# A two-layer graph attention kernel: the write of q's halves and the load of the next tile's q stack are issued at a later place of SyncE's queue

## The chip, the cores and the metric

The kernel runs on one core of a Trainium2 chip. The core has a matrix engine (TensorE: PE for matmuls, PEld for the loads of their stationary operand), a vector engine (VectorE, DVE), a scalar engine (ScalarE, ACT), a general-purpose engine (GpSimd, POOL), and SyncE (SP), which here only issues DMAs. Each engine runs its own list of instructions in order and waits on semaphores for the others. DMAs are issued from SyncE's queue (q1 in the profile) and from GpSimd's (q0); the bytes of both are moved by the same 16 DMA engines.

The metric is the device time of one execution in microseconds. Before the change it is 3294.1 us, the median of three executions (3287.58, 3294.10 and 3294.34). In the text a "slot" is one turn of the kernel's main loop, a "step" is one of the eight turns of the loop inside it, and "+x" is a time in us after a slot's first score matmul.

## What is computed

The reference takes node features x (16 graphs, 1024 nodes, 256 features) and an integer adjacency matrix of each graph, and applies two layers, each of which adds its output to x.

```
# layer 0: attention with 8 heads of 32
h = relu(layernorm(x))
Q, K, V = h @ Wq.T + bq, h @ Wk.T + bk, h @ Wv.T + bv        # by head
scores = where(adj == 0, -inf, Q @ K.T / sqrt(32))
x = x + (softmax(scores) @ V) @ Wo.T + bo

# layer 1: attention of one head, its scores chosen by the kind of the edge
h = relu(layernorm(x))
e_k = leaky_relu((h * a_k) @ h.T, 0.2)                       # k = 0..3
scores = e_0 where adj == 1, e_1 where 2, e_2 where 3, e_3 where 4, else -9e15
x = x + softmax(scores) @ h
```

The adjacency given here holds zeros and ones. The kernel notes while it runs whether any other kind occurs, and only then computes layer 1 a second time for all kinds.

## The kernel before

**Slots.** A graph (the batch index b) has 8 tiles of 128 query nodes, so there are 128 tiles. The main loop is a software pipeline over slots s. In slot s, `now` is the tile s whose attention is computed; `was` and `gone` are the two tiles before it, whose output is being finished; `nxt` is tile s + 1, whose inputs are being fetched; `edge` and `edge_was` are tiles of layer 1, which runs nine tiles behind; `piece`, `piece_was` and `piece_nxt` are tiles of the projections, which run about nine tiles ahead. In slot s, `piece_was` is tile s + 8. The loop over h inside a slot has one step for each head. The order of the instructions is written by hand (`tc.manual_schedule()`): on each engine and each queue they run in the order of the program.

**The projections.** For each piece the keys and queries are projected in two chunks of 128 output features (`project`, line 261). ScalarE then writes the result, rounded to a type that TensorE reads in one pass, into the first half of a `halves` buffer (`high`, line 277), and VectorE writes the remainder into the second half (`split`, line 282). The tag `halves` has four buffers: two are used for the keys of a piece and two for its queries. The key halves are made at the end of step 7 and split at steps 0 and 1 of the next slot. The query halves are made at step 5 and split at step 6.

The halves go to DRAM. The keys are written twice, by SyncE's queue right at the split and by GpSimd's a little later (line 309), into `kd`. The queries are written by `write_queries` (line 303) into `qd`, once for each chunk, with each half repeated: 256 KB a DMA. Before the change it is called at step 7.

**Loads.** For the scores of a tile, TensorE needs the q stack `qt`: 128 partitions (32 head dimensions by high and low half by two copies) by 8 heads by 128 queries, 512 KB in pieces of 512 bytes. `load_queries` (line 390) reads it from `qd` on SyncE's queue into one of two buffers. Before the change it is issued for `nxt` at step 1. The stack of tile s + 1 is loaded in slot s, and the halves that were made in slot s belong to tile s + 8. The keys of a whole graph (eight loads of 512 KB, line 344) stay in place for eight slots. The next graph's are loaded on GpSimd's queue during the last slot of a graph and the first of the next: one at step 3, one at the end of step 4, one at the start of step 5, one at the end of step 6, then at steps 0, 2, 3 and 4. GpSimd's queue also loads the adjacency tile (line 394, 512 KB, step 4).

**Scores and softmax.** At each step TensorE computes the scores of one head (line 423, two matmuls), VectorE adds the mask and takes the row extremum (line 435), and ScalarE takes the exponential (line 443).

**Turning the probabilities.** For the product with V the probabilities of a head must lie transposed. Heads 2, 3, 6 and 7 are transposed by TensorE (line 543) and copied by ScalarE (line 544). Heads 0, 1, 4 and 5 (`BY_BLOCKS`) take another way: VectorE transposes blocks of 32 by 32 (line 364), and four DMAs of 128 KB on SyncE's queue (line 369, `place_blocks`) move the blocks to their partitions in a buffer `pT`. Head h is turned two steps after its scores, so heads 0 and 1 are moved at steps 2 and 3 and heads 4 and 5 at steps 6 and 7. The edge tile's probabilities are moved the same way at step 0.

**The products.** `combine(0)` (line 478; 64 matmul instructions of a call in the profile) multiplies heads 0 to 3 with V at step 7, after the scores of head 7. `combine(1)` does heads 4 to 7 at step 3 of the next slot. `gather` (line 609) does the same for the edge tile at steps 5 and 6, and its result leaves through `store`: VectorE's `ot` (line 618) and SyncE's DMA `out` (line 619), at step 6. The residual row goes out at step 6 as well (`x1d`, line 504).

**SyncE's queue in a slot.** Because a queue runs in order, the order of its DMAs matters for the change. In the kernel before, from step 0 on, it is: one key write, four moves of the edge tile, one key write, the q stack, four moves of head 0, four of head 1, the output, four moves of head 4, the residual row, four moves of head 5, two q writes. That is 27 DMAs, and the profile shows about 0.6 us of the queue for each.

Of the kernel before, what the change touches and what calls it, by code (L numbers as in the profile page):

```python
# [42 lines left out]
def gnn_kernel(  # L43
# [138 lines left out]
    class Piece:  # L182
# [116 lines left out]
                self.queries.append((oc, halves))  # L299

        def write_queries(self):
            for oc, halves in self.queries:
                nc.sync.dma_start(
                    out=qds[self.b][self.first, oc].rearrange("p u w n -> p u (w n)"),
                    in_=halves.unsqueeze(1).to_broadcast([P, 2, 2 * P]),
                )
# [34 lines left out]
    def load_key(b, h):  # L341
        kt = keys.tile([P, N], F32R, tag=f"k{h}", name=f"k{h}_{b}")
        c, r = divmod(h, GROUP)
        (nc.sync, nc.gpsimd)[b > 0].dma_start(
            out=kt.bitcast(F32),
            in_=kds[b][c, r * HD : (r + 1) * HD].rearrange("d w u n -> (d w u) n"),
        )
        keysets.setdefault(b, {})[h] = kt
# [178 lines left out]
    def norms(tile_0, piece):  # L527

        both = [(a, x) for a, x in ((tile_0, tile_0 and tile_0.x1), (piece, piece and piece.x[:, 0, :])) if a]
        if both:  # L530
            mv = stats_place(len(both))
            for i, (_, xt) in enumerate(both):
                stats_of(xt, mv[:, i, :])
            r, shift = norm_of(mv)
            for i, (a, _) in enumerate(both):
                a.norm = r[:, i : i + 1], shift[:, i : i + 1]
# [151 lines left out]
    def attend_of(s):  # L688
        return Attend(*divmod(s, NT)) if 0 <= s < B * NT else None

    def edges_of(s):
        s -= LAG
        return Edges(*divmod(s, NT)) if 0 <= s < B * NT else None

    def piece_of(s):
        s += LEAD
        return Piece(*divmod(s, NT)) if s < B * NT else None

    with tc.manual_schedule():
        first = [Piece(0, 0, 4), Piece(0, 4, 4)]  # L700
        piece_was = Piece(1, 0)
# [6 lines left out]
        nxt = attend_of(1)  # L708
# [16 lines left out]
        piece, edge, edge_was = piece_next, None, None  # L725
# [6 lines left out]
            piece_was.project(0, oc)  # L732
            piece_was.high()

        gone = was = None
        for s in range(B * NT + LAG + 1):
            b, t = divmod(s, NT)

            def load_keys(h, end):
                if t == NT - 1 and b + 1 < B and 2 * h + end in KEY_STEPS:  # L740
                    load_key(b + 1, KEY_STEPS.index(2 * h + end))
                if t == 0 and 0 < b < B and 2 * (HEADS + h) + end in KEY_STEPS:
                    load_key(b, KEY_STEPS.index(2 * (HEADS + h) + end))

            nxt2, edge_nxt, piece_nxt = attend_of(s + 2), edges_of(s + 1), piece_of(s + 1)
            for h in range(HEADS):
                ending, eh = (now, h - 1) if h >= 1 else (was, HEADS - 1)
                turning, th = (now, h - 2) if h >= 2 else (was, HEADS + h - 2)

                load_keys(h, 0)  # L750


                if now:
                    now.scores(h)
                if h == 0 and piece_was:
                    piece_was.split()
                if h == 1 and piece_was:
                    piece_was.split()
                if h == 2 and edge:
                    edge.softmax_max()  # L760
                if h == 5:
                    if was:
                        was.residual()
                    norms(was, piece_nxt)
                if h == 6 and edge_was:
                    edge_was.gather(1)
                if h == 6 and piece_was:
                    piece_was.split()
                    piece_was.split()
                if now:  # L770
                    now.softmax_max(h)
                if h == 6 and edge_was:
                    edge_was.store()
                if h == 4 and edge:
                    edge.leak()


                if ending:
                    ending.softmax_exp(eh)

                if h == 1 and gone:
                    gone.turned_normed()


                if h == 3:
                    if piece_was:
                        piece_was.project(1, 0)
                        piece_was.project(1, 1)
                    if was:
                        was.combine(1)  # L790
                    if piece_was:
                        piece_was.biased()
                    if was:
                        was.combined()
                if turning and th in BY_BLOCKS:
                    turning.turn_blocks(th)
                    turning.place_blocks(th)
                elif turning:
                    turning.turn(th, 0)
                    turning.turn(th, 1)  # L800


                if h == 0:
                    if piece_was:
                        piece_was.write_again()
                    if edge:
                        edge.score(0)
                    if gone:
                        gone.turn_normed()
                    if edge_was:  # L810
                        edge_was.turn_blocks()
                        edge_was.place_blocks()
                if h == 1:
                    if edge:
                        edge.score(1)
                    if was:
                        was.reciprocals()
                    if piece_nxt:
                        piece_nxt.load()
                    if piece_was:  # L820
                        piece_was.write_again()
                    if nxt:
                        nxt.load_queries()
                if h == 2:
                    if piece_was:
                        piece_was.values()
                    if was:
                        was.turn_reciprocals()
                        was.turned_reciprocals()
                        was.add_bias()  # L830
                    if edge_was:
                        edge_was.load_nodes()
                if h == 3:
                    if nxt:
                        nxt.flag()
                        nxt.mask()
                if h == 4:
                    if was:
                        was.output()
                    if piece:  # L840
                        piece.normed()
                    if edge_nxt:
                        edge_nxt.prepare()
                    if nxt2:
                        nxt2.load()
                if h == 5:
                    if edge_was:
                        edge_was.gather(0)
                    if piece:
                        piece.turn()  # L850
                    if piece_was:
                        piece_was.high()
                        piece_was.high()
                    if piece:
                        piece.turned()
                if h == 6:
                    if edge:
                        edge.softmax_exp()
                    if was:
                        was.keep()  # L860
                    if now:
                        now.load_nodes()
                    if piece:
                        piece.project(0, 0)
                        piece.project(0, 1)
                if h == 7:
                    if now:
                        now.combine(0)
                    if piece_was:
                        piece_was.write_queries()  # L870
                    if piece:
                        piece.high()
                        piece.high()
                    if was:
                        was.normed()
                load_keys(h, 1)
            gone, was, now, nxt = was, now, nxt, nxt2
            edge_was, edge = edge, edge_nxt
            piece_was, piece = piece, piece_nxt


        seen = small.tile([P, B], F32, tag="seen", bufs=1)
# [49 lines left out]
```

## Time and profile before

| what | value |
|---|---|
| median of three executions | 3294.1 us |
| the profiled execution | 3310.8 us, its span 3309.0 us |
| mean granted TensorE clock | 0.979 of full speed |
| PE busy | 3080.0 us, 93% of the span |
| VectorE busy | 2802.7 us, 85% |
| ScalarE busy | 2458.4 us, 74% |
| GpSimd busy | 1735.3 us, 52% |
| DMA | 762.93 MB, 231 GB/s; q1 takes 55.3% and q0 19.9% of the 16 engines' span |

Busy time is the time in which an engine runs instructions; waiting for semaphores and issuing DMAs is not counted. A row of a group gives the line, the engine, the operation, what it writes and reads, how often, then the busy time and the mean ns of one, then the idle time of the engine just before these instructions and what ended most of it. A row of a DMA issue gives the size and the median time from issue to landing. A row of the timeline gives the start, the duration, the engine, the line, the operation and how many were merged, with the idle time before them in brackets. A row of the stage table gives a stretch of time, its length, the busy time of PE, PEld, VectorE, ScalarE and GpSimd, then the granted clock, the share of the 16 DMA engines that was busy, and GB/s.

### The profile page before, as it was taken

How to read it: one execution, taken by the hardware profiler on the slowest of the kernel's cores; microseconds unless marked ns; L12 is line 12 of the kernel's file. 1: busy time of each engine (PE TensorE's matmuls, PEld its weight loads, DVE VectorE, ACT ScalarE, POOL GpSimd, SP SyncE). 2: the span in 40 equal slices, each digit the busy share in tenths (PEclk: the TensorE clock that was granted, in tenths of full speed). 3: DMA queues.
4: the chain of work that ended last, by engine and by line, in shares of the span. 5: the costliest groups of instructions: out<-in, count | busy, mean ns of one | idle time of the engine just before them, and what ended most of it. 6: DMA issues, size and time to landing. Idle time of an engine off the chain costs nothing. (4 is left out here: it accounts for less than half of the span.)

```text
span 3309.0 us, 98026 instructions
## 1 busy us (share of the span) xinstructions
PE 3080.0 (93%) x36018; PEld 2239.0 (68%) x36018; DVE 2802.7 (85%) x5111; ACT 2458.4 (74%) x4829; POOL 1735.3 (52%) x3902
## 2 busy tenths in 40 slices
PE   4888999999999999999999999999999999998997
PEld 2666767777676767767677677776766676676653
DVE  2887989989898989989899888989988899898963
ACT  2887878778787877878778777878777788787750
POOL 2555555555555555555555555555555555555531
PEclk9898999999999999999999999999999999999999
DMA  5777787877878787787878878787787877877642
GB/s 187 219 232 227 235 262 221 269 225 235 264 221 267 225 254 241 223 261 228 255 229 240 245 229 253 228 261 237 229 257 218 250 235 231 252 231 242 197 136 70
DMA packets 747063, 762.93 MB, mean 231 GB/s; under 512 B 71280, under 2 KB 692080, under 8 KB 746576
## 3 DMA queue, kind: packets, MB, share of 16 engines
q1 hardware_dynamic: 678288, 542.21, 55.3%
q0 software_dynamic: 65088, 210.16, 19.9%
q8 instruction: 290, 4.75, 0.6%
q10 hardware_dynamic: 3200, 4.19, 0.3%
q14 instruction: 197, 1.61, 0.1%
HBM read 252.98 MB, written 167.77 MB: 127 GB/s over the span
## 5 line engine op out<-in xcount | busy, mean ns | idle before, releaser
L435 DVE CUSTOM_DVE_ANT_0 p<-s,neg 128x1024 f32<-128x1024 f32 x1024 | 1233.6, 1205 | 150.6 <-issue 120.5
L443 ACT ACTIVATE p<-p,nmx 128x1024 f32<-128x1024 f32 x1024 | 1178.4, 1151 | 221.2 <-DVE nmx L435 219.7
L423 PE MATMUL s<-k,qt 128*128 128x512 f32 x2048 | 797.3, 471 | 21.8 <-DVE nmx L435 9.8
L478 PE MATMUL acc<-pT,v 128*32 128x128 f32 x16384 | 561.0, 283 | 112.3 <-DMA pT<-blocks 110.7
L544 ACT COPY pT<-trp 128x512 f32<-128x512 f32 x1024 | 543.8, 582 | 162.6 <-PE trp L543 151.9
L403 POOL TENSOR_SCALAR neg<-adj 128x1024 bf16<-128x1024 int32 x128 | 467.0, 3648 | 359.3 <-ACT neg L415 358.9
L364 DVE STREAM_TRANSPOSE blocks<-p 128x1024 f32<-128x1024 f32 x512 | 632.2, 1235 | 0.1
L478 PEld LDWEIGHTS acc<-pT,v 128*32 128x32 f32 x16384 | 472.1, 114 | 196.8 <-issue 119.4
L543 PE MATMUL trp<-ident,p 128*128 128x128 f32 x4096 | 534.2, 274 | 0.2 <-ACT pT L544 0.2
L543 PEld LDWEIGHTS trp<-ident,p 128*128 128x128 f32 x4096 | 481.0, 141 | 74.0 <-ACT pT L544 3.6
L609 PE MATMUL acc<-h,pT 128*32 128x256 f32 x8192 | 509.9, 383 | 12.5 <-DMA pT<-blocks 11.8
L565 PE MATMUL s<-h1T,ha 128*128 128x512 f32 x1024 | 482.8, 595 | 0.5 <-ACT h1T L522 0.5
L423 PEld LDWEIGHTS s<-k,qt 128*128 128x128 f32 x2048 | 331.1, 192 | 155.0 <-issue 107.7
L609 PEld LDWEIGHTS acc<-h,pT 128*32 128x32 f32 x8192 | 246.6, 110 | 228.5 <-issue 78.0
L462 POOL COPY wide<-rec 128x256 f32<-128x256 f32 x128 | 51.0, 398 | 573.3 <-DVE rec L460 573.3
L309 POOL DMA_DIRECT2D kd<-halves x240 | 169.6, 707 | 238.6 <-DVE halves L282 230.6
L579 DVE CUSTOM_DVE_ANT_0 sel<-s,neg 128x1024 f32<-128x1024 f32 x128 | 156.8, 1225 | 146.2 <-PE s L565 146.2
L565 PEld LDWEIGHTS s<-h1T,ha 128*128 128x128 f32 x1024 | 175.3, 191 | 130.0 <-issue 128.6
L591 ACT ACTIVATE sel<-sel,nmx 128x1024 f32<-128x1024 f32 x128 | 145.5, 1137 | 70.8 <-DVE rec L616 64.9
L443 ACT ACTIVATION_READ_ACCUMULATOR p<-p,nmx 128x1 f32 x1024 | 193.7, 189 | 0.0
L472 ACT COPY recT<-acc 128x256 f32<-128x256 f32 x128 | 47.8, 373 | 176.7 <-PE acc L468 176.7
L261 PEld LDWEIGHTS acc<-hT,wkT 128*128 128x128 f32 x960 | 119.5, 195 | 76.1 <-issue 46.9
(106 smaller groups left out, 4008.3 us busy)
## 6 DMA issues: line engine op xcount, KB each, us to landing
pT<-blocks SPq DMA_DIRECT2D x2560, 128.0 KB, 3.5
qt<-qd SPq DMA_DIRECT2D x128, 512.0 KB, 5.5
adj<-in_adj POOLq DMA_DIRECT2D x127, 512.0 KB, 4.8
qd<-halves SPq DMA_DIRECT2D x240, 256.0 KB, 3.2
k<-kd POOLq DMA_DIRECT2D x120, 512.0 KB, 7.0
kd<-halves SPq DMA_DIRECT2D x240, 128.0 KB, 3.8
kd<-halves POOLq DMA_DIRECT2D x240, 128.0 KB, 3.6
xb<-in_x POOLq DMA_DIRECT2D x128, 128.0 KB, 3.0
```

The source lines that it names most:

```text
L309: queue.dma_start(out=kds[self.b][oc, :, :, twice, self.cols], in_=halves.rearrange("p (w n) -> p w n", w=2),)
L364: nc.vector.transpose(blocks.rearrange("p b j q -> p j b q"), p)
L403: nc.gpsimd.tensor_scalar(self.neg, self.adj, 0.0, MASKED, ALU.is_equal, ALU.mult)
L423: nc.tensor.matmul(self.ps[:, cols], lhsT=self.qt[:, h, :], rhs=keysets[self.b][h][:, cols], start=True, stop=True,)
L435: nc.vector.tensor_tensor_reduce(out=p, in0=sides[h in (3, 5, 7)], in1=self.neg, scale=-SCALE, scalar=FLOOR, op0=ALU.add, op1=ALU.min, acc ...
L443: nc.scalar.activation(p, p, AF.Exp, bias=nmx, scale=-1.0, accum_out=self.sums[:, h : h + 1])
L478: nc.tensor.matmul(sums_place[r * HD : (r + 1) * HD, g * P : (g + 1) * P], lhsT=vs[self.b][:, j, place_of(h) : place_of(h) + HD], rhs=self ...
L543: nc.tensor.transpose(tr[:, j, :], p[:, jj * P : (jj + 1) * P], ident)
L544: copy(pT[:, half * 4 : half * 4 + 4, :], tr)
L565: nc.tensor.matmul(self.e[:, cols], lhsT=self.ha[:, c, :], rhs=h1Ts[self.b][:, c, cols], start=(c == 0), stop=(c == NC - 1),)
L579: nc.vector.tensor_tensor_reduce(out=self.sel, in0=self.e, in1=masks[self.b, self.t], scale=-1.0, scalar=3e38, op0=ALU.add, op1=ALU.min, a ...
L609: nc.tensor.matmul(sums_place[a * HD : (a + 1) * HD, :], lhsT=self.pT[:, j, a], rhs=h1s[self.b][:, j, :], start=(j == 0), stop=(j == NT - 1),)
```

## The change

`write_queries` is no longer called at step 7 of the slot that made the halves. It is called at step 3 of the slot after, right behind the moves of head 1's blocks, for the piece that was `piece_was` one slot ago (`piece_gone`). `load_queries` is no longer called at step 1 but at step 3, directly behind that write and ahead of the mask's two instructions. The loop over a piece's queries now empties the list as it goes.

SyncE's queue in a slot is then: one key write, four moves of the edge tile, one key write, four moves of head 0, four of head 1, two q writes, the q stack, the output, four moves of head 4, the residual row, four moves of head 5. No instruction is added to any engine, and no buffer or size changes.

```diff
         def write_queries(self):
-            for oc, halves in self.queries:
+            while self.queries:
+                oc, halves = self.queries.pop(0)
                 nc.sync.dma_start(
...
-        gone = was = None
+        gone = was = piece_gone = None
...
                     if piece_was:
                         piece_was.write_again()
-                    if nxt:
-                        nxt.load_queries()
                 if h == 2:
...
                 if h == 3:
+                    if piece_gone:
+                        piece_gone.write_queries()
                     if nxt:
+                        nxt.load_queries()
                         nxt.flag()
                         nxt.mask()
...
                 if h == 7:
                     if now:
                         now.combine(0)
-                    if piece_was:
-                        piece_was.write_queries()
...
-            piece_was, piece = piece, piece_nxt
+            piece_gone, piece_was, piece = piece_was, piece, piece_nxt
```

## The prediction

> **What bounds the kernel now.** I read the page's engine shares first, then the list of waits (TensorE's, then SyncE's queue), then the timeline of two slots, then the stage table. A slot is one turn of the main loop (one query tile); its start is its first score matmul, and "+x" is us after that.
>
> ```profile
> PE 3080.0 (93%) x36018; PEld 2239.0 (68%) x36018; DVE 2802.7 (85%) x5111; ACT 2458.4 (74%) x4829; POOL 1735.3 (52%) x3902
> ...
> L478 PE MATMUL acc<-pT,v 128*32 128x128 f32 x16384 | 561.0, 283 | 112.3 <-DMA pT<-blocks 110.7
> ...
> pT<-blocks SPq DMA_DIRECT2D x2560, 128.0 KB, 3.5
> qt<-qd SPq DMA_DIRECT2D x128, 512.0 KB, 5.5
> ```
>
> TensorE is the bound; its one large wait is `combine` (L478) waiting for the moves of blocks. SyncE's timeline shows who is ahead of those moves. An ordinary slot (start 1062.93), then the last slot of a batch, "key slot" (start 1009.12), and TensorE's answer in it:
>
> ```profile
> 1067.50 1.21 SPq L303 DMA_DIRECT2D qd<-halves  x2
> 1068.80 0.58 SPq L309 DMA_DIRECT2D kd<-halves  x1
> 1069.48 3.62 SPq L369 DMA_DIRECT2D pT<-blocks  x4
> 1073.21 0.55 SPq L309 DMA_DIRECT2D kd<-halves  x1
> 1073.86 0.57 SPq L390 DMA_DIRECT2D qt<-qd  x1
> 1074.53 5.26 SPq L369 DMA_DIRECT2D pT<-blocks  x8
> 1084.00 0.60 SPq L619 DMA_DIRECT2D out<-ot  x1
> ```
>
> ```profile
> 1019.83 0.57 SPq L390 DMA_DIRECT2D qt<-qd  x1
> 1020.50 8.21 SPq L369 DMA_DIRECT2D pT<-blocks  x8
> ...
> 1034.95 3.63 PE L478 MATMUL acc<-pT,v 128*32 128x128 f32 x62 [4.21 <-DMA pT<-blocks]
> ```
>
> The eight moves of heads 0 and 1 stand directly behind the 512 KB stack load. In the key slot the stack lands 8.3 us after issue, at 1028.15, and the eighth move is issued at 1028.17: each of SP's DMAs waits for the one eight places ahead. That move lands 6.5 us later, at 1034.7, and `combine(0)` waits for it. The stage table shows what else the stall costs and where DMA has room:
>
> ```profile
> 1081.00:1083.00 2.00, 2.00 (x35) 1.16 (x28) 1.83 (x5) 2.00 (x6) 1.45 (x8) 1.00 0.89 293
> 1083.00:1085.00 2.00, 2.00 (x38) 1.64 (x41) 1.91 (x5) 2.00 (x5) 1.42 (x8) 1.00 0.04 14
> ```
>
> ```profile
> 1025.00:1030.00 5.00, 5.00 (x69) 3.01 (x62) 4.64 (x13) 4.48 (x12) 4.24 (x14) 1.00 1.00 327
> 1030.00:1035.00 5.00, 0.79 (x8) 0.22 (x9) 3.82 (x6) 3.37 (x7) 4.18 (x13) 0.83 0.97 329
> 1035.00:1038.50 3.50, 3.50 (x62) 3.13 (x62) 0.00 (x0) 0.00 (x0) 0.00 (x0) 0.50 0.87 253
> ```
>
> In the ordinary slot the DMA engines fall idle (0.04) from +20 to +22. In the key slot they are full (0.97 to 1.00), and after the stall the granted clock is 0.50: 62 matmuls take 3.63 us, against 2.03 us for 64 in the ordinary slot. So 4.2 us of waiting cost 6.2.
>
> **What there is to win.** A slot without a wait takes 23.18 us. Measured from the starts of the score matmuls, 84 ordinary slots (neither first nor last of a batch) are on average 0.68 longer: 57 us. Fifteen slots (14 last slots, and the one at 249.5) are 6.1 longer: 92. Thirteen first slots of a batch are 1.65 longer: 21. Together 171 us. The slots before and after these hardly wait for moves.
>
> **Part by part.**
> *Load of the q stack, from step 1 to step 3.* No instruction is added. Heads 0 and 1's moves lose 0.6 us of SP's issue and the 512 KB ahead of them. Their blocks are ready at +10.6 and +13.5 (the transposes at 1072.26 and 1075.21, 1.23 us each), so the moves now start at those times and the last is issued at +15.4. A move lands in 3.5 us: +19, and `combine(0)` starts at +21.2. In the key slot only one key load (at +10.4) is beside them; even 5.6 us would do. So the 171 us is taken off whole.
> *Write of q's halves, from step 7 to step 3 of the next slot.* Two DMAs of 256 KB, 1.2 us of SP. What stood behind them (key write, edge moves) is issued 1.2 us earlier; the edge moves are used at +15.1, so this is worth nothing. Now they precede the stack: issued +16.0 and +16.6, the stack at +17.3. Behind these three stands SP's output store, which in the ordinary slot is issued at +21.1 anyway (it waits for VectorE's `ot`): 3.2 us of cover. The stack of the tile written now is read seven slots later, so there is no data wait.
> *The halves' buffers.* Four rotate. ScalarE writes the next q halves at +17.45 (1080.38), when the write of the old ones, issued +16.6, is in flight (3.2 us: until +19.8). If the same buffers came up, ScalarE would stall 2.4 us a slot, and the key projection and two VectorE splits behind it. In the program as compiled before, buffers of a tag go in the order in which they were given back (the seven of pT: 4, 5, 6, 0, 2, 1, 3); the key halves are given back at steps 0 and 1, so q's should take theirs, and the key halves at +21.9 take q's. I price it at nothing and keep the stall as a rival.
> *Where the wait goes.* The stack must land before the next slot's first scores, +23.1: 5.8 us after issue, where it had 12. Its landing is the unknown. Low end: 4.5 us, the fastest of the trace: no wait. High end: 8.1, the median of the key slots' loads, with one 512 KB key load issued within 0.8 us: 2.3 us of wait a slot. The adjacency load, the same 512 KB, is issued on GpSimd's queue at +16.65, 0.7 before the stack, so beside it. What takes me toward the low end is the packets of the stage above: the adjacency load occupies the engines from +18 to +20, then they idle. By the trace's packet records a 512-byte packet takes 27 ns and one of 1 KB 46 ns; the stack is 64 of the first on each engine (1.7 us), a move 8 of the second (0.37 us). At +18 SP's ring then holds about 0.3 us of q writes and the stack, 2.0 us. In before, a ring holding three moves (1.1 us) at that point had landed them 3.1 us later, and one with five (1.9 us) 3.9 to 4.9 later. So the stack lands at +22 to +23.4: I take 0.2 us an ordinary slot: 84 x 0.2 = 17 us.
> *Key slots.* Two key loads go out on GpSimd right behind the adjacency load (1026.35), 1.5 MB from +18 to +24.5. SP's DMAs issued then land 6.5 to 7.1 us later for 128 KB (the moves at 1028.17 and 1033.25). The stack, four times that, lands between +25.4 (8.1 us) and +29: a wait of 2.3 to 5.9, plus up to 1.6 at the half clock. I take 4.0: 15 x 4.0 = 60. First slots have one key load (+16.8) beside adjacency: +24.6 or so, and the old waits for keys: 13 x 2.0 = 26.
> Sum: -171 + 17 + 60 + 26 = -68 us. The profiled execution is 3310.8 us, 16.7 above the median of 3294.1; taken off the median, 3226 us.
>
> Two rules speak to this, and no term above uses them. The Trainium skill, "DMA: Bandwidth & Descriptors", section "Queues, rings and completion order", says that each DMA engine takes turns between queues packet by packet. That speaks against the change: the stack's 512-byte packets would give the 4 KB packets of the adjacency load a full turn each and wait for all of it, some 1.5 us more; the ordinary slots would then cost about 84 x 1.2 = 100 us and the sum would be +15. "TensorE: Matmul & The Clock Gate", section "What's actually happening", puts the halving of the clock at an idle window of about 3.4 us; the new waits in key slots lie on both sides of that, and by it a wait of 2.4 us would cost nothing beyond itself.
>
> **Rivals.**
> *A, the forecast:* most of the wait of `combine` gone, a small one for the stack in its place: 3200 to 3270. Chance 0.42.
> *B, the stack is always in time,* in key slots too (below 2 us there): -171 + 10 to 45: 3130 to 3165. For it: 0.04 of DMA use from +20 to +22. Against: full engines in key slots. 0.13.
> *C, ends slower: the stack comes late in every slot.* Place: the first scores. It decides from 6.8 us of landing on: a 1.0 us wait in 84 slots is 84, and with 60 and 26 the 171 are spent. With 7.3 us (median of the first slots' loads, which have key loads beside them) and key slots as long as now: -171 + 126 + 92 + 40 = +87: 3381; with 8.1, 3448. For it: all loads with a 512 KB neighbour issued up to 3 us earlier took 7 us or more. Against: those rings were full, this one is drained. 0.31.
> *D, the buffers:* ScalarE stalls 2.4 us for the q write in 118 slots: +283 - 68: 3509. 0.07.
> *E, one wait for another:* within 0.2% (about what a measurement of this kernel can tell from no change), 3288 to 3301. 0.07.
>
> **Numbers.** Faster is A and B, 0.55; same is E, 0.07; slower is C and D, 0.38. The time is A's, 3226. The range leaves out D, the upper third of C and the lower part of B: 3160 to 3410; A's own range is 3200 to 3270.
>
> **What would show it.** Right: the row of L478 waiting for pT falls from 110.7 to below 15; stack issues sit at +17 with a median landing of 5 to 6 us; a new wait of L423 for qt, of some us in key slots and under 0.5 in others. Wrong: a median landing near 7 or more and L423 waiting in every slot (C); ScalarE's q halves (L277) waiting for the write of qd (D); L478 still waiting for heads 0 and 1, which would mean that the load ahead was not what held them.

## The result

The changed kernel takes 3440.6 us (median of four executions, 3431.6 to 3447.8); the kernel before took 3294.2 beside it (four, 3287.6 to 3301.1). The ratio is 1.0443, with a 95% interval of 1.041 to 1.0476. The prediction of 3226 us, faster, was wrong; what came is the case that it called C: the stack is late in every slot.

From the page of the changed kernel: the engines' busy shares, then three groups (line, engine, operation | busy time and mean ns | idle time before it and what ended it), then DMA issues with the median us from issue to landing. Lines behind the change have moved down by one (L423 is L424, L478 is L479).

```profile
PE 3087.0 (90%) x36018; PEld 2242.0 (65%) x36018; DVE 2814.4 (82%) x5111; ACT 2463.4 (72%) x4829; POOL 1729.8 (50%) x3902
...
L424 PE MATMUL s<-k,qt 128*128 128x512 f32 x2048 | 801.6, 473 | 244.0 <-DMA qt<-qd 215.2
...
L479 PE MATMUL acc<-pT,v 128*32 128x128 f32 x16384 | 514.7, 275 | 2.7 <-DMA pT<-blocks 1.9
...
L277 ACT ACTIVATE halves<-acc,bk_t 128x128 fp32r<-128x128 f32 x240 | 86.5, 362 | 129.2 <-DMA qd<-halves 124.8
...
pT<-blocks SPq DMA_DIRECT2D x2560, 128.0 KB, 2.9
qt<-qd SPq DMA_DIRECT2D x128, 512.0 KB, 6.8
adj<-in_adj POOLq DMA_DIRECT2D x127, 512.0 KB, 5.4
qd<-halves SPq DMA_DIRECT2D x240, 256.0 KB, 5.6
```

The wait that the change aimed at is gone: `combine` waited 110.7 us for moves and waits 1.9 now. In its place the scores wait 215.2 us for the q stack. TensorE's busy time hardly changed (3080.0 to 3087.0); the span grew from 3309.0 to 3429.7.

By slots, in excess of the 23.18 us of a slot without a wait, for the 110 slots from 9 to 118 in both traces:

| slots | before | after |
|---|---|---|
| 84 ordinary | 57.0 | 132.3 |
| 13 last of a graph (key slots) | 78.0 | 71.7 |
| 13 first of a graph | 21.4 | 69.5 |
| all 110 | 156.5 | 273.5 |

That is 117.0 of the 120.7 us by which the span grew. SyncE's timeline of one ordinary slot of the changed kernel (its first score matmul at 1147.99):

```profile
1162.41 1.91 SPq L370 DMA_DIRECT2D pT<-blocks  x3
1164.37 1.30 SPq L304 DMA_DIRECT2D qd<-halves  x2
1165.71 0.62 SPq L391 DMA_DIRECT2D qt<-qd  x1
```

The order is the one that was foreseen, and the times are within 0.4 us of it: last move at +15.7, q writes at +16.4 and +17.0, stack at +17.7. GpSimd issues the adjacency load in this slot at 1164.63, +16.6. The stage table of the same slot (length; busy time of PE, PEld, VectorE, ScalarE, GpSimd; granted clock; share of the DMA engines that was busy; GB/s):

```profile
1164.00:1166.00 2.00, 2.00 (x28) 1.01 (x24) 1.90 (x6) 1.48 (x5) 1.69 (x5) 1.00 0.79 218
1166.00:1168.00 2.00, 2.00 (x35) 1.11 (x28) 1.84 (x5) 2.00 (x6) 1.43 (x8) 1.00 1.00 214
1168.00:1170.00 2.00, 2.00 (x38) 1.63 (x40) 1.91 (x5) 2.00 (x5) 1.42 (x8) 1.00 0.98 341
```

From +18 to +20 (the second row) the DMA engines are busy the whole time (1.00) and move only 214 GB/s; two microseconds later they move 341 at nearly the same share (0.98). The trace's packet records say whose time that is: from +18.5 to +20.5, SP's queue got 40 packets of 1 KB through, where it had 156 in the half microsecond before; GpSimd's 4 KB packets took 550 ns each at first and 175 at the end of it. Only then did the q writes go on, and behind them the stack's 512-byte packets (27 ns each). The stack landed at +25.5, and TensorE's timeline shows what that costs:

```profile
1173.49 1.22 PE L424 MATMUL s<-k,qt 128*128 128x512 f32 x2 [2.24 <-DMA qt<-qd]
1174.51 1.91 PE L544 MATMUL trp<-ident,p 128*128 128x128 f32 x8
1176.21 2.18 PE L566 MATMUL s<-h1T,ha 128*128 128x512 f32 x4
...
1178.37 0.71 PE L424 MATMUL s<-k,qt 128*128 128x512 f32 x2
1178.92 1.04 PE L544 MATMUL trp<-ident,p 128*128 128x128 f32 x8
1179.79 1.88 PE L566 MATMUL s<-h1T,ha 128*128 128x512 f32 x4
```

After a stall of 2.24 us the same three groups take 1.22, 1.91 and 2.18 us, and one step later 0.71, 1.04 and 1.88: the stall costs another 1.7 us. The stage table has the granted clock at 0.50 there:

```profile
1174.00:1176.00 2.00, 2.00 (x9) 1.71 (x8) 1.15 (x3) 0.40 (x1) 0.00 (x0) 0.50 0.89 261
```

### The profile page after: what moved, and what is told of

The parts are those of the page before. It is cut to its first block, busy times and chain, and to the rows that moved or that the text cites. A ratio compares the mean times of both kernels' runs of the same rounds, so it can differ in the third digit from the quotient of the medians.

```text
span 3429.7 us, 97675 instructions
## 1 busy us (share of the span) xinstructions
PE 3087.0 (90%) x36018; PEld 2242.0 (65%) x36018; DVE 2814.4 (82%) x5111; ACT 2463.4 (72%) x4829; POOL 1729.8 (50%) x3902
## 3 DMA queue, kind: packets, MB, share of 16 engines
q0 software_dynamic: 65088, 210.16, 20.1%
## 4 chain that ended last, share of the span: by engine, by line
PE 54%; DMA 26%; SPq 12%; issue 2%; DVE 1%; ACT 0%; DVEq 0%; ACTq 0%
DMA qt<-qd 25%; PE s L566 12%; PE s L424 11%; PE trp L544 10%; SPq L370 8%; PE acc L479 7%; SPq L304 4%; PE acc L261 3%; PE acc L494 3%; PE acc L329 3%; PE acc L610 2%; DMA pT<-blocks 1%; PE acc L519 1%; PE acc L469 1%; DVE blocks L365 1%
## 5 line engine op out<-in xcount | busy, mean ns | idle before, releaser
L424 PE MATMUL s<-k,qt 128*128 128x512 f32 x2048 | 801.6, 473 | 244.0 <-DMA qt<-qd 215.2
L424 PEld LDWEIGHTS s<-k,qt 128*128 128x128 f32 x2048 | 332.7, 193 | 382.6 <-issue 171.3
L544 PE MATMUL trp<-ident,p 128*128 128x128 f32 x4096 | 558.0, 281 | 0.4 <-ACT pT L545 0.4
L544 PEld LDWEIGHTS trp<-ident,p 128*128 128x128 f32 x4096 | 501.2, 145 | 75.9 <-issue 5.2
L479 PE MATMUL acc<-pT,v 128*32 128x128 f32 x16384 | 514.7, 275 | 2.7 <-DMA pT<-blocks 1.9
L566 PE MATMUL s<-h1T,ha 128*128 128x512 f32 x1024 | 506.4, 620 | 0.5 <-ACT h1T L523 0.5
L479 PEld LDWEIGHTS acc<-pT,v 128*32 128x32 f32 x16384 | 443.3, 110 | 70.7 <-DVE ot L619 38.5
L566 PEld LDWEIGHTS s<-h1T,ha 128*128 128x128 f32 x1024 | 187.2, 203 | 141.5 <-issue 140.2
L277 ACT ACTIVATE halves<-acc,bk_t 128x128 fp32r<-128x128 f32 x240 | 86.5, 362 | 129.2 <-DMA qd<-halves 124.8
```

The lines of the kernel that those rows point to most:

```text
L424: nc.tensor.matmul(self.ps[:, cols], lhsT=self.qt[:, h, :], rhs=keysets[self.b][h][:, cols], start=True, stop=True,)
L479: nc.tensor.matmul(sums_place[r * HD : (r + 1) * HD, g * P : (g + 1) * P], lhsT=vs[self.b][:, j, place_of(h) : place_of(h) + HD], rhs=self ...
L544: nc.tensor.transpose(tr[:, j, :], p[:, jj * P : (jj + 1) * P], ident)
L566: nc.tensor.matmul(self.e[:, cols], lhsT=self.ha[:, c, :], rhs=h1Ts[self.b][:, c, cols], start=(c == 0), stop=(c == NC - 1),)
```

## The experiments

The ring is what SyncE's queue has issued and the DMA engines have not yet moved. Three theories stood at the start. N, the neighbour: SP's writes and the stack are held by the adjacency load beside them. R, the ring: the stack is late because it stands behind 512 KB of writes in SP's ring. P, the place: the DMA engines have no room there for the stack at all. Beside them stood the halves' buffers (the prediction's case D). Each kernel was timed beside the kernel before.

| kernel | stack load | q write | adjacency load | us | ratio to before, 95% interval |
|---|---|---|---|---|---|
| before | step 1 | step 7 | step 4 | 3294.2 | 1 |
| changed | step 3 | step 3 | step 4 | 3440.6 | 1.0443 (1.041 to 1.0476) |
| load alone | step 3 | step 7 | step 4 | 3270.7 | 0.9914 (0.9882 to 0.9945) |
| write alone | step 1 | step 3 | step 4 | 3256.6 | 0.9879 (0.9846 to 0.9911) |
| both, adjacency late | step 3 | step 3 | step 6 | 3252.7 | 0.9859 (0.9843 to 0.9876) |
| adjacency late alone | step 1 | step 7 | step 6 | 3255.7 | 0.9877 (0.9835 to 0.992) |
| stack ahead of the write | step 3 | step 3 | step 4 | 3306.6 | 1.003 (1.0012 to 1.0049) |
| five halves buffers | step 3 | step 3 | step 4 | 3442.2 | 1.0456 (1.0378 to 1.0535) |
| adjacency, half late | step 3 | step 3 | 4 and 6 | 3315.6 | 1.007 (1.005 to 1.009) |
| adjacency in two halves | step 3 | step 3 | 4 and 4 | 3455.8 | 1.0472 (1.0435 to 1.0509) |
| stack at step 0 | step 0 | step 7 | step 4 | 3320.0 | 1.0073 (1.0046 to 1.01) |
| stack at 0, write at 3 | step 0 | step 3 | step 4 | 3225.1 | 0.9783 (0.9745 to 0.9822) |
| the same, adjacency late | step 0 | step 3 | step 6 | 3252.3 | 0.9888 (0.9865 to 0.9912) |

**One part alone.** The load moved without the write:

```diff
-                    if nxt:
-                        nxt.load_queries()
                 if h == 2:
...
                 if h == 3:
                     if nxt:
+                        nxt.load_queries()
                         nxt.flag()
```

> The stack load alone moves to step 3; q's halves are written at step 7 as before. Theory R (the ring): the stack comes late because the two q writes, 512 KB, stand right ahead of it on SyncE's ring, and are themselves held by the adjacency load; without them the stack is issued at about +16.2 instead of +17.8, lands in 5.3 to 5.8 us, by +22, and TensorE's wait for qt (215 us in the changed kernel) falls below 40: 3170 to 3230 us. Theory N (the neighbour): any 512 KB load beside the adjacency load takes about 6.7 us; it lands at +22.9 to +23.5 and waits a little in every slot: 3240 to 3310 us, qt's wait 60 to 130. Theory P (the place): the DMA engines have no room for 512 KB there at all: 6.7 us or more and about 3350 us or more.

Measured: 3270.7 us. Its waits of TensorE:

```profile
PE s L424 <- DMA qt<-qd: 46.4, 25, 5.1
...
PE acc L479 <- DMA pT<-blocks: 26.3, 29, 3.0
```

The stack is issued at +16.9 in the median ordinary slot and lands at +22.9, just ahead of the scores. It takes 5.8 us there: less than N expected (6.7), at the upper end of R's 5.3 to 5.8, and the time is in N's range. So P fails, and the write ahead is a part of the loss. The write moved without the load:

```diff
                 if h == 3:
+                    if piece_gone:
+                        piece_gone.write_queries()
                     if nxt:
...
                         now.combine(0)
-                    if piece_was:
-                        piece_was.write_queries()
```

> The write of q's halves alone moves behind head 1's moves; the stack is loaded at step 1 as before. Theories R, N and P all have the wait of combine back (about 110 us on TensorE) and no wait for qt: near before, 3280 to 3310 us. What it tells apart is the buffer: if ScalarE's wait for the q writes (125 us in the changed kernel) is a cost of its own, the time is 3320 to 3420; if it only runs beside TensorE's wait, near before. The q writes should still take 5 us or more beside the adjacency load (R and N).

Measured: 3256.6 us. TensorE waits 61.8 us for moves (110.7 before), where about 110 were expected. So each part alone makes the kernel faster, by 0.9 and by 1.2%, and the two together make it 4.4% slower: neither part makes the kernel slower by itself, and the loss comes from both being in one place.

**The neighbour taken away.** The changed kernel with the adjacency load two steps later:

```diff
                 if h == 4:
...
-                    if nxt2:
-                        nxt2.load()
...
                 if h == 6:
...
                         now.load_nodes()
+                    if nxt2:
+                        nxt2.load()
```

> The changed kernel, with the adjacency load moved from step 4 to step 6 on GpSimd's queue, behind the stack. Theory N: the q writes land in 3.0 to 3.5 us and the stack in 5.0 to 5.5, by +23; the wait for qt falls from 215 to below 60 in all, most of it in key slots: 3180 to 3260 us. Theory R: the writes ahead still hold the stack, which lands in 6 to 6.5 us; qt's wait stays over 120: 3340 to 3400 us. Theory P: no change within 1%.

Measured: 3252.7 us. From its page, and from the stage table of an ordinary slot (first scores at 1082.50, so the rows are +16 to +22 as in the table above):

```profile
qt<-qd SPq DMA_DIRECT2D x128, 512.0 KB, 4.5
adj<-in_adj POOLq DMA_DIRECT2D x127, 512.0 KB, 6.0
```

```profile
1098.50:1100.50 2.00, 2.00 (x28) 1.01 (x24) 1.90 (x6) 1.48 (x5) 1.15 (x4) 1.00 0.82 234
1100.50:1102.50 2.00, 2.00 (x35) 1.11 (x28) 1.84 (x5) 2.00 (x6) 1.45 (x8) 1.00 0.91 265
1102.50:1104.50 2.00, 2.00 (x38) 1.64 (x40) 1.91 (x5) 2.00 (x5) 1.42 (x8) 1.00 0.67 201
```

With the same DMAs in the ring, issued within 0.2 us of the same times, the stack takes 4.5 us and lands at +22.45 in the median ordinary slot; the ordinary slots lose 0.13 us each (1.58 in the changed kernel). So with the write and the stack in place, the loss goes when the neighbour goes: any one of the three taken out ends it (3270.7, 3256.6, 3252.7). The control, the kernel before with only the adjacency load moved, tells how much of this the move is worth anyway:

> The kernel before with the adjacency load alone moved from step 4 to step 6: the control for the run in which it was moved in the changed kernel. In before it meets only the last moves of head 1. If its late place is worth something by itself (it lets those moves land), 3240 to 3280 us, and then the gain of that run is not the stack's alone; if not, within 0.5% of before, 3280 to 3310.

Measured: 3255.7 us. In the kernel before the edit is worth 1.2% (1 - 0.9877), in the changed kernel 5.8% (1.0443 - 0.9859). The difference, 4.6% or some 150 us, belongs to the meeting of the adjacency load with the write and the stack: as much as the change lost. It also shows what the change is worth without that meeting: nothing that can be measured (3252.7 with it, 3255.7 without it, both with the late load), for the late load alone takes the ordinary slots' loss from 0.68 to 0.18 us. The trace of the kernel before says, too, that it had the same trouble in a smaller form. In four slots running (40 to 43) its last move of head 1 went out at +16.8, +16.2, +17.5 and +15.6 and landed at +22.2, +20.2, +22.9 and +18.3: 2.7 us for the earliest, 3.9 to 5.4 for the other three.

**The dose.** The adjacency load in two halves by columns, the first at step 4, the second at step 6:

```diff
         def load(self):
             self.adj = work.tile([P, N], I32, tag="adj", bufs=1)
-            (nc.gpsimd if self.b + self.t else nc.sync).dma_start(
-                out=self.adj, in_=mixed(adj[self.b, self.rows, :])
+            self.load_half(0)
+
+        def load_half(self, i):
+            cols = slice(i * HALF, (i + 1) * HALF)
+            (nc.gpsimd if self.b + self.t else nc.sync).dma_start(
+                out=self.adj[:, cols], in_=mixed(adj[self.b, self.rows, cols])
             )
...
                         now.load_nodes()
+                    if nxt2:
+                        nxt2.load_half(1)
```

> The changed kernel with the adjacency load in two halves of 256 KB (columns 0 to 511 and 512 to 1023): the first stays in step 4, the second goes out in step 6. If the stack is held for as long as GpSimd's bytes ahead of it take (theory N), half the bytes hold it about half as long: the stack takes 5.3 to 5.8 us, between the 6.7 of the changed kernel and the 4.4 with the whole load late, and the time falls between 3440 and 3253: 3300 to 3370. If it is the start of GpSimd's load that holds SP's ring, whatever its size, the stack still takes 6.3 or more and the time stays above 3390.

Measured: 3315.6 us. The issue rows of its page, and those of the kernel with both halves at step 4:

```profile
qt<-qd SPq DMA_DIRECT2D x128, 512.0 KB, 5.7
adj<-in_adj POOLq DMA_DIRECT2D x254, 256.0 KB, 4.1
```

```profile
qt<-qd SPq DMA_DIRECT2D x128, 512.0 KB, 7.1
adj<-in_adj POOLq DMA_DIRECT2D x254, 256.0 KB, 4.9
```

With half the bytes beside it the stack takes 5.5 us in the median ordinary slot, between 4.4 (none) and 6.7 (all): what holds it goes by GpSimd's bytes, as N expected (5.3 to 5.8), and the time is in N's range. The second kernel has the same `load_half`, but the second half follows the first at once:

```diff
                     if nxt2:
                         nxt2.load()
+                        nxt2.load_half(1)
```

> The changed kernel with the adjacency load in the same two halves, both in step 4: the same bytes at the same place, in 2 KB rows instead of 4 KB. If the queues share an engine packet by packet, SP's small packets get twice as many turns: the stack lands 0.4 us or more earlier and the time falls to 3380 to 3415. If it is the bytes or the start of the load, the stack takes 6.5 to 7.1 and the time is 3425 to 3460.

Measured: 3455.8 us; the stack takes 6.9 us in ordinary slots. The finer pieces bring nothing. But this run can't decide how the queues share an engine, because the edit didn't change what it was meant to change: the trace records GpSimd's packets at 4096 bytes there too, four on each engine for a half. Between +18.5 and +20.5 SP's queue got 35 to 72 packets of 1 KB per half microsecond through, against 20 to 22 in the changed kernel, and still the whole took as long.

**The order of write and stack.** Both at step 3, the stack first:

```diff
                 if h == 3:
+                    if nxt:
+                        nxt.load_queries()
                     if piece_gone:
                         piece_gone.write_queries()
                     if nxt:
-                        nxt.load_queries()
                         nxt.flag()
```

> The changed kernel with the stack load ahead of the two q writes at step 3. Theory R: the stack is issued at +16.2 with nothing ahead but moves, lands by +22, qt's wait below 60; the q writes land later, at +24 or after, and ScalarE's wait for their buffers grows from 125 to 200 us or more; time 3200 to 3300 us if that wait is hidden. Theory N: the stack takes 6.7 us still and lands at +23: a small wait in each slot, 3280 to 3350. Theory P: as the changed kernel, 3400 to 3450.

Measured: 3306.6 us. The group rows of its page that speak:

```profile
L277 ACT ACTIVATE halves<-acc,bk_t 128x128 fp32r<-128x128 f32 x240 | 88.0, 367 | 327.0 <-DMA qd<-halves 215.5
...
L282 DVE SCALAR_TENSOR_TENSOR halves<-acc,bk_t,halves 128x128 fp32r<-128x128 f32 x240 | 79.4, 331 | 150.1 <-ACT halves L277 147.4
```

The stack takes 6.4 us and lands at +23.5, as N expected and not R; its wait falls to 39.1 us, but the q writes land at +24.7 instead of +22.6, and ScalarE waits 215.5 us for their buffers and VectorE behind it. The 512 KB that the adjacency load pushes back are late for somebody either way.

**The buffers.** The changed kernel with a fifth buffer for the halves:

```diff
-            bufs = {"p": 4, "blocks": 3, "halves": 4, "qt": 2, "xin": 2}.get(tag, 1)
+            bufs = {"p": 4, "blocks": 3, "halves": 5, "qt": 2, "xin": 2}.get(tag, 1)
```

> The changed kernel with five buffers of q's and k's halves in place of four, so that the key halves at step 7 need not wait for the q writes in flight. ScalarE's wait for qd (125 us) falls below 30. If that wait is part of what made the change slow, the time falls by 40 to 110 us, to 3330 to 3400; if it lay beside TensorE's wait for the stack, the time stays within 0.6% of the changed kernel, 3420 to 3460, and the wait for qt stays at 200 us or more.

Measured: 3442.2 us. From its waits:

```profile
PE s L424 <- DMA qt<-qd: 216.6, 114, 6.5
```

```profile
ACT halves L277 <- DMA qd<-halves: 30.9, 34, 4.1
```

ScalarE's wait falls from 124.8 to 30.9 us and the time doesn't move, nor the wait for the stack. The buffers are not the cause. The kernel with the write alone agrees: there ScalarE waits 151.2 us for the writes, and the kernel is faster than before.

**The stack early.** With the stack at the start of step 0 in place of step 1 (the kernel before, so the write is at step 7) and in place of step 3 (the changed kernel, the write at step 3):

```diff
+                if h == 0 and nxt:
+                    nxt.load_queries()
                 if h == 0 and piece_was:
                     piece_was.split()
...
                     if nxt:
-                        nxt.load_queries()
```

> The kernel before, with the stack load alone moved from step 1 to the start of step 0, ahead of both key writes and of the edge tile's moves; q's halves are written at step 7 as before. If what hurts is who stands ahead of whom on SyncE's ring (the stack ahead of heads 0 and 1's moves in before, two q writes ahead of the stack in the changed kernel), then the stack here is issued at about +6, lands by +12, is early by 11 us, and only the edge moves stand behind it, which have 7 us of room: no wait for qt, combine's wait below 40 us: 3180 to 3240 us. If it is the amount of traffic that the engines carry in steps 0 to 2, the moves of heads 0 and 1 stay late: 3270 to 3310.

> As the run with the stack at step 0, and the q writes at step 3 behind head 1's moves. The q writes are then the only 512 KB of SyncE's beside the adjacency load and nothing of TensorE's waits for them; they land by +22.5, and ScalarE waits about 150 us for their buffers, which the run with the write alone moved hid. The stack is issued earlier still, at about +4.7. 3170 to 3230 us, below the run with the stack at step 0 by 0 to 40. If ScalarE's wait for buffers costs something once TensorE waits no more, it is above it instead.

Measured: 3320.0 and 3225.1 us. With the write at step 7 it is slower than before, which I had not expected. SyncE's timeline and then TensorE's in an ordinary slot of it (first scores at 1161.85):

```profile
1167.60 1.23 SPq L303 DMA_DIRECT2D qd<-halves  x2
1168.93 0.58 SPq L390 DMA_DIRECT2D qt<-qd  x1
...
1170.55 2.91 SPq L369 DMA_DIRECT2D pT<-blocks  x4
1173.56 0.57 SPq L309 DMA_DIRECT2D kd<-halves  x1
1174.24 5.59 SPq L369 DMA_DIRECT2D pT<-blocks  x8
```

```profile
1184.95 1.95 PE L478 MATMUL acc<-pT,v 128*32 128x128 f32 x62 [1.33 <-DMA pT<-blocks]
```

The writes and the stack, 1 MB, stand directly ahead of the moves. The last move of head 1 goes out at +17.4, into the adjacency load, and lands at +23.0; `combine` waits. That is the ordinary slots' part, 20 us more than before; the key slots gained 66, and the first slots of a graph lost 67, in whose median the stack took 11 us. With the write behind the moves, in the other kernel (first scores at 1134.96):

```profile
1145.97 6.01 SPq L370 DMA_DIRECT2D pT<-blocks  x8
1152.02 1.49 SPq L304 DMA_DIRECT2D qd<-halves  x2
```

```profile
1156.18 2.02 PE L479 MATMUL acc<-pT,v 128*32 128x128 f32 x64
```

The last move goes out at +15.6 and lands at +19.2, and `combine` starts without a wait. Only the q writes meet the adjacency load, and nothing of TensorE waits for them: ordinary slots lose 0.17 us and key slots 0.14. This is the fastest version, 2.2% faster than before. What is left in it are the first slots of a graph, 5.5 us each. The same kernel with the adjacency load at step 6:

> The stack in step 0, the write of q's halves in step 3 of the next slot (which took 3225 us), and the adjacency load in step 6. In that kernel the adjacency load meets only the q writes, for whose landing no TensorE work waits: if so, moving it is worth little, 3205 to 3235. If the late load is worth the 38 us that it was worth in the kernel before, 3187.

Measured: 3252.3 us, slower than either case allowed. The load now runs from +23.0 to +28.9, which is +5.7 of the next slot, beside heads 4 and 5's moves and the edge tile's; the stack behind these goes out at +6.1 (+5.4 with the load at step 4) and takes 6.1 us (4.9). The scores wait 21.2 us for keys (8.1), and that is most of the 15.2 us between the two profiled spans. The other 12 of the 27 us between the medians are not explained by these traces. The late load is not good in itself: it moves the meeting to other transfers.

## Why the prediction was wrong

*Load from step 1 to step 3: right.* The last moves go out at +15.5 to +15.7 (+15.4 was predicted), and the row of `combine` fell below the 15 us that it named. But the price was that of both parts: with the load alone 26.3 us of the wait stay.

*Write from step 7 to step 3: right in place.* In the median ordinary slot the q writes go out at +16.4 and +17.05 (+16.0 and +16.6), the stack at +17.8 (+17.3).

*The halves' buffers: right price, wrong reason.* "Q's should take theirs" failed: ScalarE does wait, 124.8 us. It costs nothing that can be measured, as the fifth buffer shows; why it stays hidden no run tells. With the stack first, where the writes land 2 us later, the wait grows to 215.5 us; what it costs there was not tried.

*Where the wait goes: this step failed*, in the sentence "At +18 SP's ring then holds about 0.3 us of q writes and the stack, 2.0 us". Counted in the changed kernel's packet records, the median of 84 ordinary slots has 455 packets of 1 KB still ahead of the stack's at +18. The two writes are 512 such packets: most of them had not gone. The first of them went at +17.8, 1.45 us after its DMA was issued. Most of that time is no queue: where SP's ring was idle, as ahead of the output store in 79 slots of the kernel before, the first packet came 1.26 us after the issue, too. At 46 ns on 16 engines 455 packets are 1.3 us and not 0.3, so the ring held 3.0 us with the stack, not 2.0.

The pairs of ring and landing in that step were too kind as well. Counted by packets, the eleven ordinary slots of the kernel before that had 1.0 to 1.2 us of moves left at +18 landed their last move 3.8 to 5.2 us later (3.1 was taken for 1.1), and two with 2.1 and 2.3 us landed it 5.6 and 6.0 later. A straight line through its 42 slots with over 0.6 us gives, as an estimate, +23.7 for the 2.0 us that were counted and +25.1 for 3.0; measured, +24.6. So the step had both the ring and the price of the neighbour too low: even its own 2.0 us would have been a wait of about 0.6 us in 84 slots, 50 us in place of 17. With the adjacency load away, 513 packets in the ring at +18 landed the stack at +22.45: it is the neighbour that turns this ring into a wait.

Of the measured 132.3, some 112 is the delay of the next slot's first scores and 19.7 are matmuls at half clock at the slots' own beginnings, a term that the prediction had for key slots alone.

*Key slots: too low, inside their bounds.* 5.5 us each, where 4.0 was taken between 2.3 and 7.5; the stack lands at +28.2 (+25.4 to +29 was given). *First slots: 5.3 us instead of 2.0.* A first slot begins behind a key slot's stall: 2.2 us of the 5.3 are its own first matmuls at half clock. Its stack is issued at +20.1 and lands at +28.7, not "+24.6 or so", and the delay of the scores behind it is 2.1.

| term | predicted | measured |
|---|---|---|
| old excess taken off | -171 | -157 (slots 9 to 118) |
| ordinary slots | +17 | +132 |
| key slots | +60 | +72 |
| first slots | +26 | +70 |
| sum | -68 | +117 |

Another 26 us are no step's fault: the medians differ by 146.4, the profiled executions by 120.8, since the one of before stood 16.7 above its median and the one after 9.0 below.

*The rivals.* C had the mechanism, a stack that is late in every slot, and its condition ("from 6.8 us of landing on") was met: 6.8 on the page. Its sum with 7.3 us was 3381; the rest lies mostly in the first slots and in that scatter. D's wait came without its price. "Against: this ring is drained" is what spoke for A over C, and it was the miscount above. The argument that the engines idled from +20 to +22 was true of before, and did not carry: the 1 MB of write and stack could only start to fill that gap once the adjacency load was through.

*The two rules.* The Trainium skill, "DMA: Bandwidth & Descriptors", section "Queues, rings and completion order", has each engine drain one ring's packet, several descriptors at a time, before it turns to the next ring. The prediction, which took one record for one turn, weighed it at 100 us in ordinary slots, nearer to the 132 than its own 17. The trace agrees in outline: in the slot shown 92 records of 4 KB went through between +18.5 and +20.5, and SP's queue nearly stood, with 40 records of 1 KB. That fits turns of several descriptors; it does not show them. "TensorE: Matmul & The Clock Gate", section "What's actually happening", names an idle window of about 3.4 us for the fall to half clock. Here 2.24 us were enough, as shown above, so the prediction's "cost nothing beyond itself" did not hold.

## What to carry to other kernels

Before a transfer is moved later, count what is in its queue and not yet through at that time from the packet records, beginning with the first packet and not with the issue: here no move, write or store of SP's began sooner than 1.1 us after its issue. Then list what the other queues issue in the same microseconds; two moves that each gain can lose together when they bring a write, a load and a neighbour's load into one place, and taking the neighbour away, or half of it, tells it within one run. The best place for a transfer is where its landing is needed last: here the write, for which no TensorE work waits, belongs beside the adjacency load, and the stack far from it.

## What the runs showed of the hardware

*The clock fell after some stalls of 1.7 to 3.45 us, and not after others.* After a stall ahead of a slot's first scores, the next 14 matmul instructions take 3.16 us at full clock and 4.5 to 6.1 where it has fallen (most often 4.8). Over five of the kernels ("changed", "five halves buffers", "both, adjacency late", "adjacency, half late" and "adjacency in two halves") the slots 9 to 118 sort so:

| stall, us | slots | of these at half clock |
|---|---|---|
| 0.5 to 1.8 | 224 | 1 |
| 1.8 to 2.7 | 79 | 49 |
| 2.7 to 3.45 | 24 | 17 |
| over 3.45 | 51 | 51 |

In the changed kernel the excess of those instructions over 3.16 us is some 53 us in all, beside the 215 of waiting. A stall below 1.8 us cost itself alone (but for one), one above 3.45 always 1.3 us or more besides, and between the two it fell either way. Why the border lies there, no run here tells.

*One queue's load nearly stopped another's.* While GpSimd's 512 KB load ran, SP's packets of 1 KB fell from about 155 per half microsecond (adjacency late, +18 to +19) to about 21 (changed, +18.5 to +20.5), and all queues together moved 69 to 109 KB per half microsecond from +18.5 to +20, where 154 to 177 were moved just after (means over the ordinary slots). In the ordinary slots the first sixteen 4 KB packets of the load took 566 ns each on average in the changed kernel, and its last sixteen 165. The q writes seem to have a part in it: with these issued just ahead of the whole load the first sixteen took 519 to 566 ns (changed, five buffers, write alone, stack at 0 with write at 3), with no q write there 293 to 363 (before, load alone, stack at step 0, stack ahead of the write). But they are not all of it: with the load at step 6 the first sixteen took 438 to 467. What makes them slow is open; splitting the load by columns did not change the time.
